# Even and odd channels of the last two heads exchanged by two transfers instead of a matrix product

## The chip, the core and the metric

The kernel runs on one core of a Trainium2 chip. The core has five engines, each with an instruction queue of its own that it takes strictly in order: PE (TensorE, matrix products; its weight loads are shown apart as PEld), DVE (VectorE, elementwise work, scans and reductions), ACT (ScalarE, activation functions and copies), POOL (GpSimd) and SP (SyncE, which here issues nearly all of the DMAs). [...] Operands lie in SBUF, 128 partitions wide; PE writes its results to PSUM, in banks of 128 x 512 floats. A DMA copies between SBUF and DRAM, or within SBUF, beside the engines' work.

The metric is the time of one execution on the device in microseconds, as the median of several runs.

## The reference, cut to what matters

The model has two layers, each of an attention-like part and a feed-forward part, on 8 sequences of 512 tokens with 256 channels. The change lies in the first part of the first layer. There, six heads of 64 channels go through a recurrence over time, in which pairs of channels (even, odd) are rotated by angles:

```
def _rotate(x, ang):
    cos, sin = jnp.cos(ang), jnp.sin(ang)
    xe, xo = x[..., ::2], x[..., 1::2]
    ye = xe * cos - xo * sin
    yo = xo * cos + xe * sin
    return jnp.stack([ye, yo], axis=-1).reshape(x.shape)
...
def step(state, inp):
    th, ps, ph, vt, at, bt = inp
    retained = _rotate(state, ph) * at[..., None]
    write = _rotate(vt, ps)
    new_state = retained + bt[..., None] * write
    out_t = _rotate(new_state, -th)
    return (new_state, out_t)
...
rms = jax.lax.rsqrt(jnp.mean(jnp.square(out), axis=-1, keepdims=True) + EPS)
o = out * rms * rms_w * jax.nn.silu(g)
x = x + o.reshape(B, T, VALUE_DIM) @ Wo
```

The kernel takes the rotations together: values are rotated once, by the angle psi - theta of their own time step, and what remains is a plain scan over time with the decay alpha. To rotate a row of values, the row of the other member of its pair is needed.

## The kernel before

**Layout.** A sequence's values are a tile v of three parts of 128 partitions x 512 tokens. Part 0 holds the even channels of heads 0 to 3 (4 heads x 32 pairs), part 1 their odd channels. So for these heads even and odd lie on the same partitions, in different parts, and elementwise operations reach both. Part 2 holds the last two heads: their 64 even channels on partitions 0 to 63, their 64 odd ones on 64 to 127. [...] The angles of part 2 are made with opposite signs in the two halves (matrix twice), so that one addition serves both: rotated = v * cos + (v with its halves exchanged) * sin.

**One sequence of the first stage** is an object of class Sequence0, with one method for each step. Those around the change, in the order of their data:

- values(k) makes part k of v: a product with wv, then a causal convolution of four taps (ACT at L376, three DVE steps at L379).
- heads_gates (L468) makes alpha and beta, sends them to DRAM (L474) and has them spread over the partitions by four SP transfers (L359).
- written(m) multiplies v by beta (L493): m = 0 for parts 0 and 1 at once, m = 1 for part 2.
- rotated(m) rotates: m = 0 for parts 0 and 1 (L502 to L505), m = 1 for part 2 (L508 to L511). For m = 1, PE multiplies v's part 2 by the constant matrix other, an identity rolled by 64 columns, which puts the exchanged rows into a PSUM tile po (L508). DVE multiplies v by cos into u (L509), po by sin into w (L510) and adds both (L511).
- scanned(m) runs the recurrence as DVE scans (L518), one per part, and squares each result on ACT (L519): m = 0 parts 0 and 1, m = 1 part 2.
- squares(k) sums the squares over the channels of each head on PE (L525, tile pss), one product per part.
- root_means: ACT takes the root (L529), SP sends it through DRAM (L532, L533), DVE takes the reciprocal (L534), SP sends that to DRAM (L535) and spreads it (L359, tile scale); DVE multiplies o by the gates (L538).
- scaled (L542), projected_out (L548, L556), then the second norm, the router (logits, choices, ranks) and the scattering of rows to the experts.

The tiles u and w have one buffer each (bufs=1), v has two. PSUM tiles named pp, of which po is one, share four banks.

**Order.** What sets the order of work is a score of times. STEPS gives each step's due times relative to its sequence's start, STARTS the starts of the eight sequences (0 to 292, some 42 apart); all pieces are sorted by start plus due time and issued in this order (L696 to L729). Within a sequence, the entries of interest are:

```
"written": [6.5, 18.7],
"rotated": [20.9, 24.0],
"scanned": [24.4, 25.2],
"squares": [31.8, 31.9, 32.0],
"root_means": [35.0],
```

Due times are a plan for sorting; they are not the times of the trace, in which a sequence's steps come later. For PE the order of issue is kept as written (manual_schedule). For the other engines, SP's queue among them, the compiler's scheduler places each instruction by its own model of when it is ready. In the trace, DVE's order therefore departs from the score: L502 of one sequence at 116.41 us goes ahead of the convolution of values(2) at 120.01, which is due earlier.

Steps of different sequences interleave: while one sequence is rotated, the router of the sequence before and the angles of the next one are under way.

The constant other is loaded at the start on SP, between cv and wab (L325).

Of the kernel before, what the change touches and what calls it, by code (L numbers as in the profile page):

```python
# [10 lines left out]
F32 = mybir.dt.float32  # L11
# [6 lines left out]
P = 128  # L18
NB, T, D = 8, 512, 256
# [4 lines left out]
HP = P // 2  # L24
NG = 8
NV = 3
# [89 lines left out]
def two_layers(ctx: ExitStack, tc: tile.TileContext, a: dict, out: bass.AP):  # L116
    nc = tc.nc
# [3 lines left out]
    def loaded(pool, name, src, shape, dtype=F32, eng=nc.sync):  # L121
        t = pool.tile(shape, dtype, tag=name, name=name)
        eng.dma_start(out=t, in_=src)
        return t
# [160 lines left out]
    pp = moe.enter_context(tc.tile_pool(name="pp", bufs=4, space=PSUM))  # L285
# [10 lines left out]
    wp = l0.enter_context(tc.tile_pool(name="l0w", bufs=1))  # L296
# [13 lines left out]
    with tc.tile_pool(name="l0t", bufs=1) as tp:  # L310
# [6 lines left out]
        for c in range(NC):  # L317
            nc.vector.tensor_mul(wang[:, c], wka[:, c, :].unsqueeze(1).to_broadcast(full), cka)
            m = tp.tile(full, F32, name="m")
# [2 lines left out]

    wv = loaded(wp, "wv", a["wv"].rearrange("(c p) m -> p c m", p=P), [P, NC, NV * P])
    cv = loaded(wp, "cv", a["cv"].rearrange("(k p) j -> p k j", p=P), [P, NV, KW])
    other = loaded(wp, "other", a["other"], [P, P])  # L325

    wab = loaded(wp, "wab", a["wab"].rearrange("(c p) m -> p c m", p=P), [P, NC, P])
    wg = loaded(wp, "wg", a["wg0"].rearrange("(c p) m -> p c m", p=P), [P, NC, NV * P])
# [8 lines left out]
    for b in range(1, NB):  # L337
# [8 lines left out]
            out=xs[NE * REG : NE * REG + NE * P, :].rearrange("(n p) d -> p n d", p=P),  # L346
            in_=zero.unsqueeze(1).to_broadcast([P, NE, D]),
# [33 lines left out]
    class Sequence0:  # L381
# [108 lines left out]
        def written(self, m):  # L490

            v = self.v[:, 2 * m : 2 + m, :]
            nc.vector.tensor_mul(v, v, self.beta[:, m : m + 1, :].to_broadcast([P, 2 - m, T]))  # L493

        def rotated(self, m):
            v, two = self.v, [P, 2, T]
            if m == 0:
                self.u = l0a.tile([P, NV, T], F32, name="u", bufs=1)
                self.w = l0a.tile([P, NV, T], F32, name="w", bufs=1)
            u, w = self.u, self.w  # L500
            if m == 0:
                nc.vector.tensor_mul(u[:, :2, :], v[:, :2, :], self.cos[:, 0:1, :].to_broadcast(two))  # L502
                nc.vector.tensor_mul(w[:, :2, :], v[:, :2, :], self.sin[:, 0:1, :].to_broadcast(two))
                nc.vector.tensor_tensor(u[:, 0, :], u[:, 0, :], w[:, 1, :], ALU.subtract)
                nc.vector.tensor_tensor(u[:, 1, :], u[:, 1, :], w[:, 0, :], ALU.add)  # L505
            else:
                po = pp.tile([P, T], F32, tag="pp", name="po")
                nc.tensor.matmul(po, other, v[:, 2, :], start=True, stop=True)  # L508
                nc.vector.tensor_mul(u[:, 2, :], v[:, 2, :], self.cos[:, 1, :])  # L509
                nc.vector.tensor_mul(w[:, 2, :], po, self.sin[:, 1, :])  # L510
                nc.vector.tensor_tensor(u[:, 2, :], u[:, 2, :], w[:, 2, :], ALU.add)  # L511

        def scanned(self, m):
# [174 lines left out]
    l0a = first_part.enter_context(tc.tile_pool(name="l0a", bufs=2))  # L688
# [47 lines left out]
    def load_weights(n, part, first):  # L736
        f = 2 * DH if n in ("v", "o") else DH
        w = wtp.tile([P, 7, f], F32, tag=f"w{n}", name=f"w{n}", bufs=1 if n == "v" else 2)
        nc.sync.dma_start(out=w[:, :2, :], in_=plain[n][part, :, : 2 * f].rearrange("p (k f) -> p k f", k=2))
        rest = w[:, 2:, :]  # L740
        kept = made[n][part].rearrange("p (k f) -> p k f", k=5)
        if not first:
            nc.sync.dma_start(out=rest, in_=kept)
            return w, None
        nc.sync.dma_start(out=w[:, 5:, :], in_=plain[n][part, :, 2 * f :].rearrange("p (k f) -> p k f", k=2))

        return w, (lambda *eng: sums(w, *eng), lambda eng=nc.sync: eng.dma_start(out=kept, in_=rest))
# [78 lines left out]
    with tc.tile_pool(name="lk", bufs=2, side="right") as lkp, tc.tile_pool(  # L826
        name="xb", bufs=4, side="right"
# [49 lines left out]
        xb, xbT, h, hT = {}, {}, {}, {}  # L877
        weights = {}
        with tc.manual_schedule(engines={ENG.PE}):
            for s in range(NBLK + 5):  # L880
# [14 lines left out]
                if s % 12 == 2 and 0 < s // 12 <= 5:  # L895
                    n, part = ((0, 0), (1, 0), ("v", 0), (0, 1), (1, 1))[s // 12 - 1]
                    w, complete = load_weights(n, part, True)
# [89 lines left out]
    with tc.tile_pool(name="big", bufs=2, side="right") as big, tc.tile_pool(  # L987
        name="a1", bufs=1, side="right"
    ) as ap1, tc.tile_pool(name="lk", bufs=1, side="right") as lkp, tc.tile_pool(
        name="a2", bufs=2, side="right"  # L990
    ) as ap2, tc.tile_pool(name="pj", bufs=1, space=PSUM) as pj, tc.tile_pool(
        name="psc", bufs=2, space=PSUM
    ) as psc, tc.tile_pool(name="ptt", bufs=2, space=PSUM) as ptp, tc.tile_pool(
        name="pz", bufs=1, space=PSUM
# [317 lines left out]
        for c in (1, 2, 4, 6):  # L1312
# [14 lines left out]
            out=mask[:, T - P :],  # L1327
            in_=mask[:, T - P :],
# [139 lines left out]
    with tc.tile_pool(name="f1", bufs=1) as f1, tc.tile_pool(  # L1468
        name="f2", bufs=2
    ) as f2, tc.tile_pool(name="f3", bufs=3) as f3, tc.tile_pool(name="ft", bufs=1, space=PSUM) as ft, tc.tile_pool(  # L1470
        name="fp", bufs=3, space=PSUM
# [196 lines left out]
```

## Time and profile before

| What | Value |
|---|---|
| median of 3 runs | 2189.84 us (2188.67 to 2193.24) |
| the profiled execution: its time, its span | 2196.19 us, 2194.3 us |
| PE, DVE, ACT, POOL busy over the span | 96%, 70%, 54%, 41% |
| first stage (0 to about 365 us), busy: PE, DVE, ACT | 328.5, 291.7, 244.6 us |
| DMA share of its 16 engines' time, 133 to 332 us | 0.19 to 0.21 |
| products with other (L508) | 8, two passes each, 592 ns a pass |
| multiplications by beta of part 2 (L493) | 8, about 0.68 us |
| L509, L510, L511 | 8 each, 687, 670 and 670 ns |
| scans (L518) | 24, 1218 ns |

The eight products of L508 start at 43.4, 86.9, 126.3, 168.5, 207.4, 245.9, 283.9 and 325.8 us: one sequence takes 38 to 44 us of the stage. Sequences are numbered 0 to 7 below.

A line of a timeline reads: start in us from the span's beginning, duration in us, engine, line of the code, operation, what it writes and reads with the shapes, and, in brackets, how long the engine was idle before it and who ended that. Several like instructions in a row are merged into one line (x2). Instructions on one engine are pipelined, so a start can lie before the last one's end.

### The profile page before, as it was taken

The page shows a single profiled execution, that of the slowest core. Times are in us where ns is not written, and L with a number is a line of the kernel's source. Part 1 is how long each engine was busy: PE and PEld are TensorE (multiplying, and loading weights), DVE is VectorE, ACT ScalarE, POOL GpSimd, SP SyncE. Part 2 cuts the span into 40 slices and gives each one's busy share as a digit, 9 for nine tenths or more (in the row PEclk, how much of TensorE's full clock was granted, in tenths as well). Part 3 has the DMA queues.
Part 4 walks back from the last instruction along what each step waited for, and adds up shares of the span by engine and source line. Part 5 has one row for each costly group of instructions (what it writes and reads, how often), then busy time and mean ns, then how long its engine had stood idle before and what let it go on. Part 6 is the DMA issues. An engine that isn't in the chain of part 4 may idle for free. (4 is left out here: it accounts for less than half of the span.)

```text
span 2194.3 us, 29865 instructions
## 1 busy us (share of the span) xinstructions
PE 2098.4 (96%) x8733; PEld 1549.3 (71%) x8733; DVE 1541.3 (70%) x3950; ACT 1182.6 (54%) x2943; POOL 899.9 (41%) x895
## 2 busy tenths in 40 slices
PE   6999999999899999999999999999999999989999
PEld 2455555786677777777777777777777777758887
DVE  6789886655667777767767766766766766857765
ACT  5776763333456556556556555556656655733211
POOL 0023223101454485576466666655535545320000
PEclk9999999999999999999999999999999999999999
DMA  6112116553477776666666666666667666520000
GB/s 199 42 69 70 68 71 219 187 165 114 131 238 236 223 225 223 217 210 223 216 214 210 214 225 211 212 214 214 208 202 225 203 218 214 160 65 10 20 20 30
DMA packets 212676, 364.02 MB, mean 166 GB/s; under 512 B 27697, under 2 KB 146865, under 8 KB 212513
## 3 DMA queue, kind: packets, MB, share of 16 engines
q1 hardware_dynamic: 202320, 333.62, 47.5%
q0 software_dynamic: 8896, 27.42, 3.8%
q8 instruction: 71, 1.16, 0.2%
q10 hardware_dynamic: 1296, 1.06, 0.2%
q14 instruction: 93, 0.75, 0.1%
HBM read 241.29 MB, written 120.72 MB: 165 GB/s over the span
## 5 line engine op out<-in xcount | busy, mean ns | idle before, releaser
L1150 ACT ACTIVATE slots<-pr,rd 128x128 f32<-128x128 f32 x756 | 302.2, 463 | 187.9 <-DVE rd L1138 121.5
L1186 PE MATMUL pz<-pT,v 128*128 128x512 f32 (+3 forms) x1024 | 302.7, 439 | 20.6 <-DMA pT<-squares 20.0
L1115 PE MATMUL sc<-qk,qk 128*128 128x128 f32 (+3 forms) x1024 | 319.0, 434 | 0.9 <-DVE low L1120 0.8
L1130 ACT ACTIVATE pr<-pr,low 128x128 f32<-128x128 f32 (+3 forms) x512 | 282.5, 553 | 58.4 <-DVE low L1120 56.9
L1186 PEld LDWEIGHTS pz<-pT,v 128*128 128x128 f32 x1024 | 192.7, 191 | 140.7 <-issue 69.1
L1120 DVE CUSTOM_DVE_ANT_0 pr<-sc,mask 128x128 f32<-128x128 f32 (+3 forms) x512 | 237.9, 483 | 68.0 <-PE sc L1115 65.4
L969 POOL TENSOR_SCALAR tmp<-idx,lut 128x344 f32<-128x344 int32 (+2 forms) x210 | 276.3, 1316 | 18.0
L1154 DVE STREAM_TRANSPOSE slots<-slots 128x1280 f32<-128x1280 f32 x126 | 190.2, 1510 | 102.9 <-ACT slots L1150 102.9
L239 PE MATMUL pb<-tT,w 128*128 128x256 f32 x762 | 208.4, 382 | 7.3 <-DVE qk L253 5.2
L632 POOL DMA_INDIRECT xs<-xn,slot x64 | 81.1, 1267 | 308.5 <-DVE share L642 122.0
L1115 PEld LDWEIGHTS sc<-qk,qk 128*128 128x128 f32 x1024 | 173.2, 191 | 47.5 <-ACT slots L1150 1.6
L1193 ACT COPY zT<-pz 128x512 f32<-128x512 f32 x128 | 74.7, 584 | 244.5 <-PE pz L1186 244.1
L239 PEld LDWEIGHTS pb<-tT,w 128*128 128x128 f32 x762 | 139.3, 190 | 29.3 <-DVE qk L253 10.0
L251 DVE TENSOR_TENSOR u<-pa,p 128x256 f32<-128x256 f32 x230 | 96.5, 420 | 78.6 <-ACT p L249 73.6
L239 PE MATMUL pa<-xT,w 128*128 128x256 f32 x508 | 151.2, 379 | 0.0
L1217 POOL TENSOR_TENSOR zS<-zT 128x512 f32<-128x512 f32 x31 | 40.6, 1310 | 265.3 <-PE po L1241 265.2
L262 DVE TENSOR_TENSOR qk<-pb,u 128x512 f32<-128x512 f32 x127 | 85.3, 672 | 90.3 <-PE pb L239 90.2
L905 POOL DMA_INDIRECT yg<-ys,yrow x64 | 65.0, 1016 | 193.1 <-PE pu L190 140.2
L1241 PE MATMUL po<-zS,wo 128*128 128x256 f32 x512 | 126.0, 380 | 1.3 <-DVE kept L1252 1.3
L252 DVE TENSOR_TENSOR p<-pb,u 128x256 f32<-128x256 f32 x230 | 97.6, 424 | 23.8 <-PE pb L239 1.1
L972 POOL TENSOR_TENSOR fs<-fs,tmp 128x344 f32<-128x344 f32 x120 | 109.7, 914 | 10.0
L239 PE MATMUL pb<-wv,tT 128*128 128x256 f32 x378 | 103.8, 384 | 8.6 <-DVE qk L262 6.9
(315 smaller groups left out, 4311.2 us busy)
## 6 DMA issues: line engine op xcount, KB each, us to landing
squares<-slots SPq DMA_DIRECT2D x504, 160.0 KB
pT<-squares SPq DMA_DIRECT2D x126, 640.0 KB
w<-sqk SPq DMA_DIRECT2D x112, 320.0 KB
w<-in_aqk SPq DMA_DIRECT2D x144, 128.0 KB
wv<-sv SPq DMA_DIRECT2D x28, 640.0 KB
wo<-so SPq DMA_DIRECT2D x28, 384.0 KB
xb<-xs SPq DMA_DIRECT2D x79, 128.0 KB
ys<-yb SPq DMA_DIRECT2D x79, 128.0 KB
```

What stands on the lines that cost most here:

```text
L239: nc.tensor.matmul(to, lhsT, rhs, start=first, stop=True, skip_group_check=True)
L251: nc.vector.tensor_tensor(self.u2, pa[:, 1, :], p1, ALU.add)
L252: nc.vector.tensor_tensor(p1, pb[:, 0, :], self.u2, ALU.add)
L969: nc.gpsimd.tensor_scalar(tmp[:k, :n], idx[:k, :n], float(v), lut[:k, v : v + 1], ALU.is_equal, ALU.mult)
L972: nc.gpsimd.tensor_add(dst, dst, tmp[:k, :n])
L1115: nc.tensor.matmul(sc[:, :kw], self.qT[:, i * P : kw], self.kT[:, :kw], start=True, stop=True)
L1120: nc.vector.tensor_tensor_reduce(out=pr, in0=sc[:, :kw], in1=mask[:, T - kw :], scale=-1.0 / math.sqrt(DH), scalar=3e38, op0=ALU.add, op1= ...
L1130: nc.scalar.activation(pr, pr, AF.Exp, bias=low, scale=-1.0, accum_out=self.den[:, i : i + 1])
L1150: nc.scalar.activation(to, pr, AF.Copy, scale=rd)
L1154: nc.vector.transpose(self.slots, self.slots)
L1186: nc.tensor.matmul(pz[:, :, j:, :].rearrange("p q i k -> p q (i k)"), self.v(j), self.pT[:, :, SLOT[j, j] : SLOT[j, j] + NT - j, :].rearra ...
L1241: nc.tensor.matmul(po[:, m, :], self.w[:, n, k * P : (k + 1) * P], self.sides[n][:, k, :], start=(k == 0), stop=(k == 1),)
```

## The change

The product with other is replaced by two SP transfers within SBUF. As soon as part 2 of v has been multiplied by beta, rows 64 to 127 of it are copied to rows 0 to 63 of w's part 2, and rows 0 to 63 to rows 64 to 127. rotated(1) then multiplies w's part 2 by sin in place. For this, u and w are allocated in written(0) instead of rotated(0). The constant other and its load go. STEPS and all other due times stay as they are.

```
-    other = loaded(wp, "other", a["other"], [P, P])
...
             v = self.v[:, 2 * m : 2 + m, :]
             nc.vector.tensor_mul(v, v, self.beta[:, m : m + 1, :].to_broadcast([P, 2 - m, T]))
-
-        def rotated(self, m):
-            v, two = self.v, [P, 2, T]
             if m == 0:
                 self.u = l0a.tile([P, NV, T], F32, name="u", bufs=1)
                 self.w = l0a.tile([P, NV, T], F32, name="w", bufs=1)
+            else:
+
+                for h in range(2):
+                    nc.sync.dma_start(
+                        out=self.w[h * HP : (h + 1) * HP, 2, :], in_=self.v[(1 - h) * HP : (2 - h) * HP, 2, :]
+                    )
+
+        def rotated(self, m):
+            v, two = self.v, [P, 2, T]
             u, w = self.u, self.w
...
             else:
-                po = pp.tile([P, T], F32, tag="pp", name="po")
-                nc.tensor.matmul(po, other, v[:, 2, :], start=True, stop=True)
                 nc.vector.tensor_mul(u[:, 2, :], v[:, 2, :], self.cos[:, 1, :])
-                nc.vector.tensor_mul(w[:, 2, :], po, self.sin[:, 1, :])
+                nc.vector.tensor_mul(w[:, 2, :], w[:, 2, :], self.sin[:, 1, :])
                 nc.vector.tensor_tensor(u[:, 2, :], u[:, 2, :], w[:, 2, :], ALU.add)
...
-        "other": np.roll(np.eye(P, dtype=np.float32), HP, axis=1),
```

## The prediction

> **What bounds the stage now.** I first read the busy time by stretch, cut at the third squares product (pss) of each sequence. The row for sequence 5 (columns: stretch, length, then busy us of PE, PEld, DVE, ACT, POOL):
>
> ```profile
> 214.30:252.30 38.00, 35.44 (x118) 19.19 (x118) 33.88 (x74) 29.22 (x42) 9.82 (x8) 1.00 0.19 68
> ```
>
> PE is busy 93%, DVE 89%. That alone suggests that PE time saved is time saved. Which wait ends last decides; so next the waits of PE, from 50 to 350 us (total, times, longest):
>
> ```profile
> PE pss L525 <- ACT sq L519: 8.9, 8, 3.6
> PE po L548 <- DVE o L542: 6.5, 7, 1.5
> ```
>
> PE stands at two fixed places per sequence, and the first lies just behind the product that the change removes. The timelines of PE, DVE and ACT show how sequence 5 gets there (start, duration):
>
> ```profile
> 245.87 1.02 PE L508 MATMUL po<-v,other 128*128 128x512 f32 x2
> 246.72 1.88 PE L190 MATMUL pp<-xT,wqkm 128*128 128x512 f32 x4
> 248.44 1.41 PE L571 MATMUL pl<-cent,xTe 128*128 128x16 f32 x12
> 249.70 1.96 PE L525 MATMUL pss<-sq,hsum 128*128 128x512 f32 x4
> 252.32 1.12 PE L525 MATMUL pss<-sq,hsum 128*128 128x512 f32 x2 [0.66 <-ACT sq L519]
> ```
> ```profile
> 244.43 0.69 DVE L493 TENSOR_TENSOR v<-v,beta 128x512 f32<-128x512 f32 x1
> 245.03 0.69 DVE L504 TENSOR_TENSOR u<-u,w 128x512 f32<-128x512 f32 x1
> 245.63 0.69 DVE L505 TENSOR_TENSOR u<-u,w 128x512 f32<-128x512 f32 x1
> 246.23 0.69 DVE L509 TENSOR_TENSOR u<-v,cos 128x512 f32<-128x512 f32 x1
> 246.83 1.22 DVE L518 TENSOR_TENSOR_SCAN o<-alpha,u 128x512 f32<-128x512 f32 x1
> 247.97 0.67 DVE L510 TENSOR_TENSOR w<-po,sin 128x512 f32<-128x512 f32 x1
> 248.55 1.22 DVE L518 TENSOR_TENSOR_SCAN o<-alpha,u 128x512 f32<-128x512 f32 x1
> 249.68 0.67 DVE L511 TENSOR_TENSOR u<-u,w 128x512 f32<-128x512 f32 x1
> 250.38 1.22 DVE L518 TENSOR_TENSOR_SCAN o<-alpha,u 128x512 f32<-128x512 f32 x1
> ```
> ```profile
> 251.64 0.63 ACT L519 ACTIVATE sq<-o 128x512 f32<-128x512 f32 x1 [0.64 <-DVE o L518]
> ```
>
> DVE runs without a gap (each row starts as the one before drains; this timeline has no idle time from 229.8 to 256.1). The third scan ends at 251.6, ACT squares it, PE starts the last pss at 252.32 after idling. So **DVE's queue from L542 (scaled) to the third scan sets this period**, not PE. Behind pss come ACT's root, SP's chain over DRAM and the spread of the scale, which DVE waits for again at L542: the loop closes over DVE, PE and DMA latency.
>
> **Removed: eight products (L508).** In sequence 5 the product occupies PE from 245.87 to the next start at 246.72: 0.85 us (the 592 ns of a record are longer, since the two passes overlap). Eight make 6.8 us of PE time. It stands ahead of pss. In sequences 2 to 7 PE idles there already (0.98, 0.77, 1.09, 0.66, 0.72, 0.71 us), in sequence 0 for 3.61. If the third scan does not end earlier, PE only reaches the same wait 0.85 us sooner, and the removal is worth nothing in these seven. What is late next is DVE's chain. The PSUM bank of po, held until L510 has read it, comes free as well; no PE wait of note names that, so 0. Sequence 1 differs (DVE):
>
> ```profile
> 88.07 0.69 DVE L510 TENSOR_TENSOR w<-po,sin 128x512 f32<-128x512 f32 x1 [1.09 <-PE po L508]
> ```
>
> There DVE waited 1.09 us for this product, and pss ran without a wait: PE and DVE both come earlier, by min(0.85, 1.09) = **0.85 us gained**. In sequences 2 and 3 the multiplication L510 stands behind layer-norm statistics that DVE took while po was not there (two bn_stats from 128.18 to 129.38 in sequence 2, one from 170.59 to 171.18 in sequence 3). If the exchanged rows come before those, the third scan is up to 1.2 and 0.6 us earlier: bounds 0 and 1.8, taken **1.2**, as the order of DVE is not written by hand and may keep them.
>
> **Added: sixteen transfers (64 rows of 2 KB, 128 KB each) on SP.** SP issues them once v is multiplied by beta (L493, second form). What is queued behind on SP is droots (L532), which the trace of SP has at 254.29, ten us after L493 of the same sequence; SP stands idle for root from the alpha spread on (183.5 us in eight waits). So neither the wait nor two issues of about 0.55 us delay anybody on SP. The landing is what matters: L510 may not start before it. No transfer from SBUF to SBUF is in the trace; the nearest rows are SP's write of root, and DVE's waits for the spread of scale:
>
> ```profile
> 254.29 0.29 SPq L532 DMA_DIRECT2D droots<-root  x1
> 255.76 0.35 SPq L533 DMA_DIRECT2D flat<-droots  x1
> ```
> ```profile
> 145.49 1.22 DVE L542 TENSOR_TENSOR o<-o,scale 128x1024 f32<-128x1024 f32 x1 [1.82 <-DMA scale<-dscale]
> 148.07 0.69 DVE L542 TENSOR_TENSOR o<-o,scale 128x512 f32<-128x512 f32 x1 [1.36 <-DMA scale<-dscale]
> ```
>
> The second droots transfer waits for the first: 1.47 us from issue to landing for 16 KB. Low end: 1.47 + 0.3 for a second issue = 1.8 us. The two scale transfers (256 KB each) were issued from 140.68; the first was there 4.81 us later, the second 2.58 after it, or 99 GB/s, which leaves 2.23 us fixed. At that rate 128 KB take 1.29 us and both are there after 2.23 + 2 x 1.29 = 4.8 us: high end. I take the fixed part of droots (it leaves SBUF, too, and reads no DRAM) plus 0.55 for the second issue plus 256 KB at 305 GB/s, a rate that the DMA view shows in the loads at the start (0.86 us): 1.47 + 0.55 + 0.86 = **2.9 us**. The source of the spread is four rows, that of the exchange 64, so its slow rate is the end that is farther off.
>
> [...] Against that stands the cover: work on DVE between the end of L493 and the start of L510. From the DVE timelines of all eight: 4.0, 5.8, 5.6, 8.1, 2.9, 2.9, 5.7, 6.2 us. [...]
>
> **Moved and small.** u and w are allocated in written(0) instead of rotated(0). Their last reader is L518 of the sequence before, over 15 us earlier: 0. The product from PSUM (L510, 0.67) becomes one from SBUF in place; L511, from SBUF, takes 0.67: 0. Regions of one tile don't wait for each other here (ACT writes v's third part at 116.60 while L502 reads the first two), so L503 and the transfers don't either. If L510 moves behind the second scan, L510, L511 and the third scan follow each other without another instruction between; dependent pairs stand 0.72 apart (88.07, 88.80, 89.52) instead of 0.58: 0.3 us a sequence in 4 to 7 at most, taken as half, **0.6 lost**. The load of other (64 KB, 0.53 us on SP at the start) goes: later loads start earlier, but PE waits there for wang, whose inputs were issued ahead of it; 0 to 0.5, taken 0.
>
> **Sum:** -0.85 - 1.2 + 0.4 + 0.6 = -1.05 us. Against the profiled execution: 2196.19 us with a span of 2194.3 becomes 2195.1. The median of the runs, 2189.84, lies 0.3% below it; nothing of that bears on stage one, so I subtract the same: **2188.8 us**. Everything behind the stage shifts with it.
>
> **Rivals.**
> *The multiplication waits for the landing.* DVE takes its queue in order, so L510 placed too early stops both scans as well. Directly behind L509 the cover is three operations of 0.6 = 1.8 us, and 2.9 - 1.8 = 1.1 us is lost in each of the five sequences whose L493 has only such operations between it and the scans (0, 1, 2, 4, 5): +5.5. With the order kept and a landing after 4.8 us: 0.8 + 1.9 + 1.9 = +4.6. So about 2195. It decides from a landing some 0.6 us beyond the cover. For it: DVE has no slack and its order will be laid out anew; against it: two scans of 1.15 us are ready to be put ahead.
> *PE is the bound after all.* All 6.8 us are gained, for which the third scan must end 0.85 us earlier everywhere: 2183. For it: 93% busy, and bn_stats between L510 and the scans in sequences 1 to 4; against it: the idle time at pss and DVE without a gap.
> *The third scan falls back.* If other work (a convolution step, 0.74 us, or bn_stats) gets ahead of L511 and the scan while the exchange is under way, 0.5 to 1 us a sequence is lost, pss idles more, +4 to +8, taken +5: 2195. For it: sequences 1 to 3 show just that; against it: in 4 to 7 little of it is ready.
>
> **Chances.** About 0.2% (4.4 us) is what a measurement of this kernel tells from no change. Forecast 0.40 (0.31 within, 0.08 faster, 0.01 slower); landing awaited 0.27 (0.24 slower, 0.03 within); PE bound 0.18 (0.17 faster, 0.01 within); scan falls back 0.15 (0.10 slower, 0.05 within). Sums: faster 0.25, within 0.40, slower 0.35. The forecast's own range is 2185 to 2192; to hold 8 in 10, with both signs, 2181.5 to 2197.5, just beyond the rivals' times.
>
> **What would show it.** PE idle at the third pss grows by about 0.85 us in sequences 4 to 7; L510 has no DMA wait, or under 0.7 us in 4 and 5; the interval from one third scan to the next stays at 38.0 and 38.7 us for sequences 4 to 5 and 5 to 6. A DMA wait of 1 us at L510 in most sequences speaks for the first rival, a shorter interval with pss idle unchanged for the second, foreign work ahead of L511 for the third. The prediction falls if the order on DVE changes elsewhere in the stage, of which this trace shows nothing.

## The result and the profile after

The change makes the kernel slower: 2200.77 us, median of 7 runs (2195.98 to 2202.68), beside 2193.39 us (2188.67 to 2199.03, 7 runs) for the kernel before on the same chip. The ratio is 1.0032, 95% interval 1.0018 to 1.0045. A second set, 12 runs of the same instructions with their order written out by hand, gave 1.0031 (1.0018 to 1.0044). The profiled execution of the change took 2195.98 us (span 2194.2). It is its fastest, while the profiled execution of before (2196.19) is one of before's slower ones, so the two spans hide the difference. What can be compared is the stage, since the change edits nothing behind it: the third squares product (pss) of sequence 7 ends at 339.98 us instead of 333.46, **6.5 us later**, near the 7.4 us between the medians. Two limits hold for everything that is read from single profiled executions. From that point to the end, the twenty traces of this case take 1853.8 to 1862.9 us (before 1860.8, the change 1854.2). And the point itself lies 2.5 us apart in two programs that differ by unread transfers only (before, and e10 below). So a difference of 2 us in one trace proves nothing by itself; the ratios of many runs decide.

The busy time by stretch (the same columns as before: stretch, length, busy us of PE, PEld, DVE, ACT, POOL, clock, DMA share, GB/s), each from the predecessor's third pss to the sequence's own, for sequence 4 and below it for sequence 5:

```profile
174.92:219.14 44.22, 38.59 (x117) 21.27 (x117) 37.67 (x80) 29.69 (x43) 9.61 (x8) 0.90 0.20 68
219.14:258.17 39.03, 35.69 (x118) 18.93 (x117) 32.01 (x71) 30.24 (x41) 10.66 (x7) 0.99 0.21 70
```

DVE was busy 33.88 us of 38.0 in sequence 5 before and is busy 32.01 of 39.0 now. Sequence 4 takes 44.22 us instead of 39.24, and the granted clock of PE in it is 0.90 in the mean, where before it was 1.00. The waits of PE from 50 to 350 us:

```profile
PE pss L528 <- ACT sq L522: 12.0, 6, 5.6
PE po L551 <- DVE o L545: 8.5, 8, 2.5
```

Both totals grew (8.9 and 6.5 us before), so PE got time off and could not use it. Third pss of all eight sequences, in us, from the PE timelines, with e1 (change, old order) for the comparison further down:

| | 0 | 1 | 2 | 3 | 4 | 5 | 6 | 7 |
|---|---|---|---|---|---|---|---|---|
| before | 54.22 | 93.66 | 134.21 | 176.16 | 215.40 | 253.44 | 292.14 | 333.46 |
| after | 56.02 | 93.40 | 133.96 | 174.92 | 219.14 | 258.17 | 298.57 | 339.98 |
| e1 | 54.42 | 93.01 | 133.36 | 175.19 | 215.41 | 254.91 | 295.28 | 336.32 |

Against this trace of before, the change is 1.8 us late after sequence 0, level after sequence 1 and 1.2 us early after sequence 3; it then loses 5.0 us in sequence 4 and 2.7 in 5 and 6. The first two of these figures flatter the change. In before's trace DVE itself waited 1.46 us for beta at L493 of part 2 in sequence 0; counted from there to the third pss, sequence 0 took 11.6 us before and 14.9 after. And before's sequence 1 was long because PE's granted clock fell in it, which the section on the prediction shows. Two places in the change's trace stand out. The first is on DVE in sequence 0:

```profile
44.59 0.69 DVE L509 TENSOR_TENSOR u<-u,w 128x512 f32<-128x512 f32 x1
45.19 0.68 DVE L510 TENSOR_TENSOR u<-u,w 128x512 f32<-128x512 f32 x1
47.98 0.69 DVE L513 TENSOR_TENSOR w<-w,sin 128x512 f32<-128x512 f32 x1 [2.10 <-DMA w<-v]
48.59 1.22 DVE L521 TENSOR_TENSOR_SCAN o<-alpha,u 128x512 f32<-128x512 f32 x1
```

L513 is the multiplication by sin that was L510. It waits 2.10 us for the transfers, which SP began to issue at 41.87: 6.1 us to the landing. All three scans stand behind it, the first two of which need nothing from it. No other L513 waits for a DMA. The second place is sequence 4, on PE (the output products of sequence 3, and the third pss of sequence 4) and in the clock by stretches of 5 us:

```profile
189.84 8.73 PE L551 MATMUL po<-wo,o 128*128 128x256 f32 x24 [2.46 <-DVE o L545]
...
217.07 2.07 PE L528 MATMUL pss<-sq,hsum 128*128 128x512 f32 x2 [2.82 <-ACT sq L522]
```
```profile
185.00:190.00 5.00, 2.54 (x12) 1.26 (x10) 2.65 (x4) 4.99 (x9) 0.00 (x0) 0.94 0.27 101
190.00:195.00 5.00, 5.00 (x12) 3.54 (x13) 3.80 (x5) 2.18 (x4) 0.00 (x0) 0.50 0.15 52
195.00:200.00 5.00, 5.00 (x21) 3.90 (x20) 4.00 (x6) 3.03 (x3) 0.00 (x0) 0.87 0.26 102
```

After a wait of 2.46 us PE runs at half its clock (0.50 from 190 to 195): the 24 products take 8.73 us, where before the same 24 took 1.10 and 4.58. Comparing the instructions of the two programs shows that the order differs too: the scheduler put 107 of the 635 DVE instructions of the stage, and 32 of ACT's 288, in another place. Presumably it did so because, without the product, it plans with other times.

### The profile page after: what moved, and what is told of

Its sections match the earlier page's. It is cut to its first block, busy times and chain, and to the rows that moved or that the text cites. A ratio compares the mean times of both kernels' runs of the same rounds, so it can differ in the third digit from the quotient of the medians.

```text
span 2194.2 us, 29874 instructions
## 1 busy us (share of the span) xinstructions
PE 2100.6 (96%) x8717; PEld 1550.5 (71%) x8717; DVE 1540.8 (70%) x3950; ACT 1183.9 (54%) x2944; POOL 895.8 (41%) x895
```

## The experiments

Three things changed at once: a product less on PE, transfers and a wait for them, another order on DVE and ACT. The experiments hold two and vary the third. (That u and w are allocated earlier is part of e1 and e6, too.) An order is held by a chain of dependences without a semaphore, written behind the list of pieces; "order of before" and "new order" below mean this block with the places of the one or the other kernel:

```
    hand = {ENG.DVE: [0, 1, 2, 3, 17, 18, 125, ...], ENG.Activation: [0, 1, 2, ...]}
    for engine, places in hand.items():
        here = [i for i in nc.cur_bb.bb.instructions if i.engine == engine]
        for earlier, then in zip(places, places[1:]):
            tc.add_manual_dep(here[then], here[earlier].name, ..., reason="order by hand")
```

All results, against runs of the kernel before on the same chip. "Stage" is the end of the third pss of sequence 7 in the one profiled execution (before: 333.46).

| run | what | stage, us | ratio (95%) |
|---|---|---|---|
| e1 | exchange, order of before | 336.32 | 1.0018 (1.0006 to 1.0030) |
| e2 | product, new order | 341.62 | 1.0042 (1.0026 to 1.0058) |
| e3 | exchange and unread product, new order | 340.21 | 1.0059 (1.0042 to 1.0077) |
| e4 | neither, new order | 335.85 | 1.0008 (0.9993 to 1.0022) |
| e5 | exchange, new order, PE kept busy | 340.26 | 1.0052 (1.0034 to 1.0071) |
| e6 | neither, order of before | 333.21 | 1.0000 (0.9990 to 1.0010) |
| e7 | exchange and unread product, order of before | 338.97 | 1.0029 (1.0016 to 1.0043) |
| e8 | product in sequence 0, exchange after, order of before | 333.07 | 1.0013 (1.0004 to 1.0022) |
| e9 | new order, third scan of sequence 4 earlier | 342.67 | 1.0031 (1.0016 to 1.0045) |
| e10 | before and unread transfers | 330.96 | 0.9997 (0.9985 to 1.0008) |
| e11 | e8, L513 later in 4 and 5 | 333.88 | 1.0001 (0.9988 to 1.0015) |
| e12 | the change again | 340.18 | 1.0031 (1.0018 to 1.0044) |
| e13 | new order, reciprocal of sequence 3 earlier | 340.04 | 1.0029 (1.0014 to 1.0043) |
| e14 | e13 and e9 | 339.06 | 1.0027 (1.0013 to 1.0040) |
| e15 | e14, product in sequence 0 | 337.16 | 1.0005 (0.9993 to 1.0016) |
| e16 | the change, product in sequence 0 | 339.99 | 1.0013 (1.0003 to 1.0023) |
| e17 | before, exchange in sequence 0 only | 336.32 | 1.0017 (1.0006 to 1.0027) |
| e18 | exchange, order of before, wide spreads | 326.37 | 0.9966 (0.9950 to 0.9982) |

### Order, product and transfers apart: e1 to e4, e6, e7

e1 is the change with the order of before, e2 the kernel before with the new order; nothing else differs.

> The exchange by transfers as in the change, but DVE and ACT take the first stage's instructions in the order that the kernel before has (the scheduler had changed 107 of 635 places on DVE and 32 of 288 on ACT). In the profile of the change the last squares product of sequence 7 ends at 340.0 us, in that of before at 333.5. Theory 'order' (the changed DVE order costs the time): ratio to before 0.998 to 1.000, that product ends at 331 to 334 us. Theory 'idle PE' (the removed products leave PE waiting longer, its granted clock drops and its work slows): ratio 1.002 to 1.004, clock under 0.98 in places between 100 and 300 us, end at 337 us or later. Theory 'landing' (DVE waits for the transfers): DMA waits of 0.5 us or more at the multiplication by sin in sequences 4 and 5, ratio 1.001 to 1.003.

> The product on PE as before, but DVE and ACT in the order that the scheduler gave the change. Theory 'order': ratio to before 1.002 to 1.005, last squares product ends at 338 to 341 us. Theory 'idle PE': ratio 0.999 to 1.001, granted clock 1.00 from 100 to 300 us as before. Theory 'landing': ratio 0.999 to 1.001.

Neither theory alone holds. The exchange costs 0.18% in the old order, and the new order costs 0.42% where the product is still there: DVE then comes to the multiplication too early and waits 1.08 to 1.33 us for the product in sequences 1, 3 and 5. The two do not add up to the change's 0.32%, since the exchange has no product to wait for. To see what each part is worth, e3 and e7 bring an unread product back, and e4 and e6 take the transfers away as well, so that these two leave the exchange out altogether:

```
+                po = pp.tile([P, T], F32, tag="pp", name="po")                       # e3, e7
+                nc.tensor.matmul(po, twice, v[:, 2, :], start=True, stop=True)
...
-                for h in range(2): nc.sync.dma_start(out=self.w[...], in_=self.v[...])  # e4, e6
...
-                nc.vector.tensor_mul(w[:, 2, :], w[:, 2, :], self.sin[:, 1, :])
+                nc.vector.tensor_mul(w[:, 2, :], v[:, 2, :], self.sin[:, 1, :])
```

> The change with its own order, and a product on PE at the place of the removed one (v by the constant twice, result not read), so that PE is as busy as before. Theory 'idle PE': the clock stays at 1.00 from 100 to 300 us, ratio to before 0.999 to 1.001. Theory 'order': ratio 1.002 to 1.005, about the change's 1.0032 or a little more. Theory 'landing': 1.003.

> The change with its own order, without the sixteen transfers: the multiplication by sin reads v itself, so even and odd channels of the last two heads are not exchanged. Theory 'landing': ratio to before 0.996 to 0.999, as both the product and its replacement are gone. Theory 'order': 1.002 to 1.004; at most the 2.1 us DMA wait of sequence 0 goes. Theory 'idle PE': 1.002 to 1.004, with a clock below 0.98 in places between 100 and 300 us.

> No product, no transfers (the sine multiplication reads v, so the last heads' channels are not exchanged), VectorE and ScalarE in the order of before. Theory 'transfers cost' (the landing and the queue's traffic are what the exchange in the old order lost): ratio 0.998 to 1.000 against before, last third sum of squares at 333 or earlier instead of 336.32, no sine multiplication waiting for a DMA. Theory 'TensorE without the product' (its cover is gone, so it waits and its clock falls): as the exchange in that order, ratio 1.0015 to 1.002, a window between 250 and 300 with a clock below 0.8.

> The exchange by transfers, with an unread product at the old place so that TensorE's program is that of before, and VectorE and ScalarE in the order of before: the kernel before plus two transfers and a wait for them. Theory 'transfers cost': ratio 1.001 to 1.0025 as without the product, sine multiplications wait for a DMA in sequences 0, 4 and 5 (2.0, 0.35, 0.30 us). Theory 'TensorE without the product': ratio 0.9995 to 1.0007, clock 1.00 in every window from 100 to 340, last third sum of squares at 333 to 334.

e6 answers the prediction's first question: with neither product nor transfers, in the old order, the ratio is 1.0000. **In the order of before the removed product was worth nothing**, within 0.1% (2.2 us) either way. It also bounds the idea in this order: what the exchange costs is a loss, as nothing stands on the other side. With e1 that cost is 0.18%. The new order without either (e4) costs 0.08%, an interval that holds 0. Putting an unread product back beside the exchange did not help: e3 is slower than the change (1.0059 against 1.0032, the intervals just overlap), e7 not clearly slower than e1. So an idle PE is not what the change suffers from. Why the product costs something in the new order, where nobody waits for it in e3, was not pursued.

### Traffic or wait: e10, e8, e11, e17, e16

e10 adds the same sixteen transfers to the kernel before, into a tile that nobody reads then:

```
+            if m == 1:
+                for h in range(2):
+                    nc.sync.dma_start(out=self.whole[h * HP : (h + 1) * HP, 0, :], in_=self.v[(1 - h) * HP : (2 - h) * HP, 2, :])
```

> The kernel before, product and all, with the two transfers of each sequence added into a tile that nobody reads then (turns, dead after the cosines), in the order of before: the queue carries the transfers, and no instruction of VectorE waits for them. Theory 'wait' (the landing on the path is what transfers cost): ratio 0.9995 to 1.0006, third sums of squares as before within 0.5 us. Theory 'traffic' (the transfers delay the other transfers or slow the engines): ratio 1.0015 to 1.002, o<-scale later by some 0.5 us in each sequence.

0.9997 (0.9985 to 1.0008): no cost of the transfers, their issues and their traffic is seen. What costs is waiting for them. In e1 DVE waited in three places: 2.02 us in sequence 0, 0.35 in 4, 0.30 in 5. e8 removes the first, with the product in sequence 0 alone (`if self.b == 0`), e11 moves L513 behind the second scan in sequences 4 and 5 as well (the places `323, 321, 324` become `323, 324, 321`, and the like).

> The exchange by transfers in sequences 1 to 7, the product in sequence 0, VectorE and ScalarE in the order of before. Theory 'the landing in sequence 0 costs': first third sum of squares at 54.2 as before, and the end of the stage 1 to 2 us earlier than the exchange in that order (336.32), ratio 1.0008 to 1.0012. Theory 'the later sequences cost' (DMA waits in 4 and 5, clock in 250 to 300): sequence 0 only regains its 2 us, which the following sequences' slack absorbs, and the ratio stays 1.0015 to 1.002.

> Product in sequence 0, transfers in 1 to 7, order of before, with the sine multiplication of sequences 4 and 5 behind the second scan instead of ahead of it (1.2 us later, where it waited 0.34 and 0.33 us). Theory 'wait': no wait for a DMA anywhere, last third sum of squares 0.5 us or more earlier than 333.07, ratio 1.0000 to 1.0007. Theory 'traffic': waits gone, ratio as before that edit, 1.001.

Without the wait in sequence 0 the stage of e8's profile ends with before's (333.07), though its ratio, 1.0013, is not clearly below e1's; without all three waits the ratio is 1.0001. The intervals of e8 and e11 overlap, so what the two short waits cost by themselves is not settled. The long one was then tried alone, in both directions: e17 puts it into the kernel before (`if self.b == 0` at the transfers, `if self.b > 0` at the product), e16 takes it out of the change as it was made.

> The kernel before in its order, with transfers in sequence 0 alone and the product in 1 to 7. Theory 'wait in sequence 0': sine multiplication waits 2.0 to 2.5 us for a DMA in sequence 0 and for none after, every third sum of squares from sequence 1 on 1 to 2.5 us later than before's, ratio 1.001 to 1.002. Theory 'two causes' (slack behind sequence 0 takes the wait back up, as the change's own sequence 1 did): ratio 0.9995 to 1.0007.

> The change in its own order, nothing moved, with the product in sequence 0 and transfers in 1 to 7. Theory 'wait in sequence 0' (it is the whole loss): first third sum of squares at 53 to 54.2, ratio 0.9997 to 1.0009 against before. Theory 'two causes' (the late reciprocal and the falling clock in sequence 4 stand beside it): first third sum of squares the same, PE's wait of 2.5 us at 189 and a clock below 0.75 after it still there, ratio 1.0013 to 1.0022.

e17, on DVE:

```profile
49.27 0.69 DVE L517 TENSOR_TENSOR w<-w,sin 128x512 f32<-128x512 f32 x1 [2.40 <-DMA w<-v]
90.30 0.69 DVE L517 TENSOR_TENSOR w<-po,sin 128x512 f32<-128x512 f32 x1 [1.10 <-PE po L515]
```

One wait of 2.40 us in the first sequence costs 0.17%, about 3.7 us (1.3 to 5.9). It makes the third pss of sequence 0 end 2.2 us later than before's, and those of the next seven are 2.2, 2.1, 2.3, 2.9, 3.1, 3.2 and 2.9 us later: **in this pair of traces nothing behind it takes it back up**. Taking the same wait out of the change brings 1.0031 down to 1.0013. So it is about half of the loss, by putting it in and by taking it out.

Two readings speak less clearly. e16's own trace shows no gain at the end: its third pss is 2.7 us earlier than the change's in sequence 0, 1.3 in sequence 4, and in sequence 7 it comes at 339.99, beside 339.98. That execution took 2198.67 us, 2.0 more than the median of its twelve; the gain rests on the medians. And between e1 and e8 the ratios differ by 0.05% only, with intervals wide enough for 0.17.

### Where the new order loses: e12, e9, e5, e13, e14, e15

e12 asks whether the loss in sequence 4 returns at all.

> The change itself a second time, with its own order written out by hand (no instruction differs): how far two executions' traces agree. Theory 'order' and theory 'clock' alike: third sum of squares of sequence 4 within 1 us of 219.14 and the last within 1.5 us of 339.98, slow output products after 189 again, ratio 1.002 to 1.0045. If the stage ends at 336 or less, the loss in sequence 4 is an accident of one execution.

It does: third pss of sequence 4 at 220.26, PE waits 2.63 and 2.87 us, clock 0.64 and 0.68 from 190 to 200. The first suspect was DVE's row in sequence 4, where two bn_stats and a convolution step stand among L513, L514 and the third scan; e9 puts those behind the scan (places `365, 321, 366, 322, 326, 325` become `321, 322, 325, 365, 366, 326`).

> The change in its own order but for six instructions of VectorE in sequence 4: the sine multiplication, the addition and the third scan go ahead of two bn_stats and one convolution step that stood before and between them (0.60 + 0.60 + 0.66 us). Theory 'order' (the third scan behind the fillers makes the stage late): third sum of squares of sequence 4 at 217.3 instead of 219.14, granted clock in 215 to 220 back to above 0.9, the last one at 337 to 338 instead of 339.98, ratio 1.0020 to 1.0027 against before. Theory 'clock earlier' (the loss of sequence 4 is TensorE's slow products at 190): 0.5 us or less at the stage's end, ratio 1.003 as the change.

A miss: third pss of sequence 4 at 220.29, ratio as before the edit. The second suspect was the clock. e5 puts products on zero weights where PE waited (`none` is a tile of zeros), ahead of this pss and, not shown, ahead of the output products of sequences 3 and 5:

```
+            if k == NV - 1 and self.b == 4:
+                for _ in range(4):
+                    nc.tensor.matmul(self.pss, none, self.sq[:, 1, :], start=False, stop=False)
```

> The change in its own order, with 14 products on zero weights (10 of 512 columns, 4 of 256, about 0.56 and 0.24 us each) put where TensorE waited before its clock fell: 4 ahead of the first output product of sequence 3 (it waited 2.46 us at 189.84), 4 ahead of the third sum of squares of sequence 4 (2.82 us at 217.07), 2 and 4 around the first output products of sequence 5 (1.50 and 1.34 us before 274.57). Theory 'clock' (the idle stretches lower the granted clock and the slow products after them cost the time): granted clock 1.00 in 190 to 200, 215 to 220 and 275 to 280, the 24 output products of sequence 3 in 5.7 us instead of 8.73, the last third sum of squares some 3 to 5 us earlier than 339.98, ratio 0.997 to 0.999 against the change itself, 1.000 to 1.002 against the kernel before. Theory 'order' (VectorE's order delays the third scans and the clock only shows it): clock 1.00 there too, but the third sums of squares end within 1 us of the change's, ratio 1.003 against before.

The clock did rise there, and fell in two places where it had been 1.00:

```profile
190.00:195.00 5.00, 5.00 (x20) 3.37 (x19) 3.64 (x5) 2.59 (x6) 0.00 (x0) 1.00 0.13 50
...
245.00:250.00 5.00, 3.11 (x10) 1.92 (x10) 5.00 (x12) 4.14 (x8) 4.39 (x3) 0.74 0.36 105
...
295.00:300.00 5.00, 5.00 (x10) 1.97 (x9) 3.85 (x5) 3.88 (x4) 3.03 (x2) 0.66 0.18 59
```

In sequence 4 itself the time came back (41.28 us from third pss to third pss, 44.22 in the change), but sequences 3, 5 and 7 took 1.2, 0.8 and 0.9 us longer. The stage ended as late as the change's (340.26), and the whole ran at 1.0052: a full clock at these places did not make the kernel faster. How much of that the added products cost is not known. What makes the output products of sequence 3 wait is seen by following the scale from the root in the change and in e1. The change:

```profile
177.24 0.35 SPq L536 DMA_DIRECT2D flat<-droots  x1
181.95 0.34 DVE L537 RECIPROCAL flat<-flat 128x32 f32<-128x32 f32 x1
...
188.47 1.23 DVE L545 TENSOR_TENSOR o<-o,scale 128x1024 f32<-128x1024 f32 x1 [0.86 <-DMA scale<-dscale]
```

And e1:

```profile
177.41 0.35 SPq L536 DMA_DIRECT2D flat<-droots  x1
179.55 0.34 DVE L537 RECIPROCAL flat<-flat 128x32 f32<-128x32 f32 x1
...
186.64 1.22 DVE L545 TENSOR_TENSOR o<-o,scale 128x1024 f32<-128x1024 f32 x1 [0.78 <-DMA scale<-dscale]
```

The same load of flat is followed 2.4 us later by the reciprocal, since the new order puts it behind five more routing instructions, and those start later. e13 moves only this reciprocal up (place 254 from behind 272 to behind 265), e14 adds e9's edit, e15 the product in sequence 0.

> The change in its own order but for one instruction: the reciprocal of flat in sequence 3 goes ahead of seven small routing instructions (0.22 us each) that stood before it. Theory 'reciprocal' (it sends the scale late, TensorE waits 2.5 to 2.8 us at the output products and runs them at a clock of 0.5 to 0.7): reciprocal at 180.7 instead of 182.44, first scaled output at 187.4 instead of 189.13, TensorE's wait there below 1.2 us, clock 1.00 from 185 to 200, 24 output products in 5.7 us instead of 8.6, third sum of squares of sequence 4 at 216 to 217 instead of 220, the last at 336 to 337.5 instead of 340.1, ratio 1.0015 to 1.0024 against before. Theory 'clock elsewhere' (a fall of the clock is only moved, as with the warm products): wait gone there, the clock below 0.8 in another window after 200, the stage's end within 1 us of 340, ratio 1.003.

> The same, with the third scan of sequence 4 also ahead of its three fillers. Theory 'reciprocal': within 0.5 us of the run before at the stage's end, as TensorE no longer comes early there. Theory 'third scan too': sequence 4's third sum of squares at 214.5 to 215.5, the stage's end 1 to 2 us before that of the run before, ratio 1.001 to 1.0018.

> The same order as the last, with the product in sequence 0 and transfers in 1 to 7: the wait for the landing in sequence 0 (2.1 to 2.4 us) is gone too. Theory 'two causes' (landing in sequence 0 and the late reciprocal are all of the loss): first third sum of squares at 53 to 54.2, the stage's end at 333 to 334.5, ratio 0.9995 to 1.0008. Theory 'a third cause': ratio 1.001 or more.

e13 did on the spot what was expected: reciprocal at 180.19, wait for the products 1.51, clock 1.00 from 185 to 200, third pss of sequence 4 at 216.39. But the gain was gone by the stage's end:

```profile
210.00:215.00 5.00, 1.95 (x4) 0.80 (x4) 5.00 (x9) 2.87 (x5) 2.25 (x3) 0.82 0.22 79
215.00:220.00 5.00, 5.00 (x9) 2.10 (x7) 1.77 (x3) 2.45 (x3) 0.00 (x0) 0.50 0.05 10
```

From 210 to 215 DVE is busy all of the time and PE 1.95 us; then PE runs at half its clock. The order seems to be late in several places, and mending one shows the next. e14 and e15 differ by the product in sequence 0 alone, 1.0027 against 1.0005, which measures the wait there a third time, at 0.22%. What the order costs beside it is 0.13% by e16 (0.03 to 0.23) and 0.08% by e4 (an interval that holds 0); **to which of its 107 places it belongs is not settled**: the two edits in e15 may have helped by 0.08%, but the intervals of e15 and e16 overlap.

### Why the landing takes 6 us, and a faster version: e18

In sequences 4 and 5 of e1 the landing came 3.27 and 3.22 us after the first issue; in sequence 0 it takes 6. The DMA view of the change from 33 to 49 us (40 slices of 0.4 us, busy tenths of the 16 DMA engines):

```profile
DMA  0000212222222222222222222999522221000000
```

and from 82 to 98 us, around the transfers of sequence 1:

```profile
DMA  0000000019990000000000000000000020003000
```

In both, the three 9s are the transfers. In sequence 0 they fall into a long run of 2s, at 102 GB/s, that goes on for 2.4 us behind them: the spreads of beta and alpha, four times 256 KB issued from 33.37 to 35.9, which at 102 GB/s last until about 46. In sequence 1 nothing else is under way. From 37 to 43 us, with the spreads alone, the share of the 16 DMA engines is 0.26 (the digit 2 is cut off, not rounded), from 43.0 to 44.2, with the transfers beside them, 0.95. The spreads read four rows each, the transfers 64. From the two shares my guess was that their few rows hold the spreads to a part of the DMA engines, and that a transfer spread over more of them is there only when its last part is, behind the spreads; e18 tests this. It lets the rows stand several times in DRAM, so that 16 rows (alpha, beta) and 8 (scale) are read:

```
-    dgates = tc.dram_tile([NB, 2 * NG, T], F32, name="dgates")
+    dgates = tc.dram_tile([NB, 2 * NG, 4, T], F32, name="dgates")
...
-                in_=rows[m * (NG // 2) : (m + 1) * (NG // 2), :].unsqueeze(1).to_broadcast([NG // 2, PAIRS, T]),
+                in_=rows[m * (NG // 2) : (m + 1) * (NG // 2)].rearrange("g c t -> (g c) t").unsqueeze(1)
+                .to_broadcast([NG // 2 * rows.shape[1], PAIRS // rows.shape[1], T]),
...
-            nc.sync.dma_start(out=d, in_=ab[: 2 * NG])
+            nc.sync.dma_start(out=d, in_=ab[: 2 * NG].unsqueeze(1).to_broadcast([2 * NG, 4, T]))
...
-            nc.sync.dma_start(out=dscale[b].rearrange("(p n) -> p n", p=P), in_=flat)
+            for c in range(2):
+                nc.sync.dma_start(out=dscale[b][:, c, :].rearrange("g (s n) -> g s n", n=NG * T // P), in_=flat)
```

> The exchange by transfers in the order of before, with the spreads of alpha, beta and scale read from rows that stand several times in DRAM (four times for alpha and beta, twice for the scale, one issue of 0.35 us more), so that the source has 16 and 8 rows instead of 4. Theory 'backlog' (in sequence 0 the transfers wait behind the packets of the alpha and beta spreads, which four rows bind to about a fifth of the DMA engines at 102 GB/s): the share of 0.2 from 35 to 46 us is gone, the spreads over before 41 us at 200 GB/s or more, the sine multiplication of sequence 0 waits 0.3 us or less instead of 2.02, first third sum of squares at 52 to 54. Theory 'other cause' (the landing is long for another reason, such as reading v just written): it still waits 1.5 us or more with the spreads over. Time: the two parts of the scale land some 1 and 2 us earlier in each sequence (2.58 us from one to the other before, some 1.3 now, less one issue); if the scale is on the stage's loop, the last third sum of squares comes 5 us or more before 333 and the ratio is 0.996 to 0.999; if VectorE's queue is the loop, 0.9995 to 1.0005.

The DMA view from 33 to 49 us, the multiplication in sequence 0, and the scale of sequence 2:

```profile
DMA  0049830000696999999810000029980000000000
```
```profile
46.45 0.69 DVE L516 TENSOR_TENSOR w<-w,sin 128x512 f32<-128x512 f32 x1
...
142.94 1.23 DVE L549 TENSOR_TENSOR o<-o,scale 128x1024 f32<-128x1024 f32 x1 [2.05 <-DMA scale<-dscale]
144.65 0.69 DVE L549 TENSOR_TENSOR o<-o,scale 128x512 f32<-128x512 f32 x1 [0.48 <-DMA scale<-dscale]
```

The spreads are over at 41.4 (digits of 6 to 9 from 37 to 41, where the change has 2), the transfers, issued at 42.52, are over at 45.0, and no wait is left in sequence 0: the backlog was the cause. The first third pss came at 54.49 all the same, since PE, after a wait of 2.98 us, took 5.50 us for the six pss products, which took 4.40 in before. The parts of the scale come 1.7 us apart on DVE instead of 2.6 (145.49 and 148.07 before), DVE's waits for it from 50 to 350 us fall from 14.1 us (e1) to 8.5, and the stage ends 7.1 us before before's. The ratio 0.9966 makes this the fastest kernel of the study. From e1 (1.0018) only the spreads differ, so they make it so, not the exchange; which of the three spreads brings how much was not separated, and the same spreads with the product in place were not tried.

## Why the prediction was wrong

**What bounds the stage: right.** The forecast took a loop for the limit: DVE's queue from L542 to the third scan, then pss, the root's way over DRAM, the spread of scale and DVE again, with the product outside of it. e6 shows the product at 1.0000. e18 shows that the spread is inside: with its landing shortened, among other spreads, the stage ends 10 us before e1's.

**Sequence 1, 0.85 us gained: not shown, and its base was an accident of the trace.** Sequence 1 took 39.44 us before and takes 38.59 in e1, exactly 0.85 less. But that is luck. In before's trace PE's clock was 0.61 from 84 to 88 us, and the products ahead of po ran slowly:

```profile
83.60 3.51 PE L190 MATMUL pp<-xT,wg 128*128 128x512 f32 x4
86.90 1.13 PE L508 MATMUL po<-v,other 128*128 128x512 f32 x2
```

e10, the same program but for unread transfers, had no such slow stretch there, the same four products taking 1.88 us:

```profile
82.31 1.88 PE L190 MATMUL pp<-xT,wg 128*128 128x512 f32 x4
84.03 1.02 PE L513 MATMUL po<-v,other 128*128 128x512 f32 x2
```

DVE did not wait for po, and sequence 1 took 37.74 us with the product in place; e6, without it and with the four products in 2.83 us, took 39.56. Over all traces, sequence 1 takes 37.2 to 37.9 us where these four products take 1.88 us, as in the change (clock 1.00 from 85 to 88), and 38.6 to 39.6 where they take 2.8 to 3.6. So the wait of 1.09 us that the forecast read as the product's price came and went with the clock.

**Sequences 2 and 3, 1.2 us gained: the mechanism came in one of the two.** In the change, L513 of sequence 3 went ahead of the statistics and the scans, and the sequence took 1.0 us less. In sequence 2 one bn_stats still stands ahead, and nothing was gained. The reading that DVE took the statistics "while po was not there" was wrong: the products had started at 126.30 and 168.46 and ended some 1.0 us later, before the statistics at 128.18 and 170.59. They stood ahead by the scheduler's order alone.

**SP and the queue: right.** e10, with all transfers and no wait for them, stands at 0.9997 (0.9985 to 1.0008).

**The landing, 2.9 us: the step that failed first.** I worked out one landing for all eight sequences and compared it with eight covers, so that only sequences 4 and 5, with 2.9 us of cover, could be exposed. There the size was fair: the landing took 3.2 to 3.3 us in e1, beside my 2.9. The 0.4 us that the sum has for the exposure is a term that no run shows; in its place e1 showed waits of 0.35 and 0.30 us in these two, 0.65 together. But in sequence 0 it took 6.1 us against a cover of 4.0, beyond even the high end of 4.8. That was to be read from the trace of before: its DMA row, too, shows the four spreads running at 102 GB/s past 46 us, while L493 of sequence 0 ends at 43.3. I used the scale's spreads, which have the same form, to bound a landing, and did not ask whether such spreads would be in its way. (My 99 GB/s for them counts 1000 bytes to the KB; with 1024, as in the 305, it is 102.) I looked for who waits behind the transfers and not for what they wait behind.

**What an exposed microsecond costs: not asked.** I priced an exposure at its own length. e17 agrees in the stage (2.4 us of wait, 2.2 to 3.2 us later in every sequence). It fits the loop: what stops DVE inside of it moves everything behind, while a product outside of it is worth nothing. e16's trace, which ends where the change's does, does not show it.

**The order on DVE: the second failing step.** "As the order of DVE is not written by hand and may keep them" admitted that the order could change, but the sum took only small shifts at L510. It changed in 107 places, the reciprocal of flat in sequence 3 among them, which is far from the edit. The prediction named this as what would bring it down. Its price beside the landing is 0.0 to 0.2%, and the places that cost stay open.

**Dependent pairs, 0.6 us lost: not seen as such.** In the sequences meant, 4 to 7, the new order has L513 ahead of the scans in 5, 6 and 7, and behind them in 4, with a bn_stats on either side. e11, where it stands behind the second scan in 4 and 5, was no slower.

**The rivals.** "The multiplication waits for the landing" had the mechanism and the sign, with another place: one wait of 2.1 us, not five of 1.1, or one of 0.8 and two of 1.9. "The third scan falls back" named bn_stats and convolution steps ahead of the scan, which the change has in sequence 4; e9 shows that they were not what cost. The clock was in none of the cases.

**The sum.** -1.05 us was forecast; the medians differ by +7.4, of which the wait in sequence 0 is about 3.7. The rest of the way from 2188.8 to 2200.77 is the base: three runs of before had a median of 2189.84, seven have 2193.39.

## What to carry to other kernels

How long a transfer takes can depend on what is still under way when it is issued (here 6.1 us to the landing behind the spreads, 3.2 to 3.3 in two later sequences of e1; with the spreads over, in e18, its traffic ended 2.5 us after the issue), so read the DMA row at each moment of issue, the first pass of a loop above all, and not the size alone. Where a loop over one engine's queue and a transfer's landing sets the period, an instruction taken from outside of it can be worth nothing (1.0000 in e6), and a stall inside of it can be paid to the end (2.4 us of wait, 2.9 us at the stage's end in e17). A wait in a single profiled execution can be an accident of the clock (1.09 us in before, none in e10): look at a second one before pricing it. An edit that changes one instruction can make a scheduler lay out a whole stage anew: compare the orders before looking for a cause, and hold the order by hand to measure the edit itself.

## What the runs showed of the hardware

Several waits of PE of 2.5 to 2.9 us were followed by a lower granted clock for some 5 us (0.50 from 190 to 195 in the change, 0.87 from 195 to 200), but not all: in e4, behind a wait of 2.64 us that ended at 187.68, the 24 output products took 1.10 and 4.58 us, as in before at a clock of 1.00. Shorter waits close together were followed by it too, at times: behind 1.51 and 0.76 us with four products between them the clock was 0.66 from 190 to 195 in e14, and behind the same waits (1.51 and 0.74) it was 1.00 in e13. In sequence 1, the same waits (1.55 us, then three of 0.16) were followed by a clock of 0.61 and four products in 3.51 us in before, and by the same four in 1.88 us in e10. So in these runs the length of a wait alone did not tell what the clock did; what else decides it was not shown. And the spreads of alpha and beta from four rows ran at 101 and 102 GB/s in before and in the change (37 to 43 us), from 16 rows at 174 to 369 GB/s (e18, slices from 37 to 41 us).
